# A switching LSTM's loads and stores move: waits in the relational sum, logit stores inside the recurrence, zero rows after the bases

## The chip, the core and the metric

The kernel runs on one core of a Trainium2 chip. The metric is the device time of one execution in microseconds (us). The engines are PE (TensorE), DVE (VectorE), ACT (ScalarE), POOL (GpSimd) and SP (SyncE). ACT, SP and POOL each have a queue on which they issue transfers (DMAs); an engine works through its instructions in the order in which they stand on it.

## The reference

A graph of 625 nodes with 512 features each and 20,000 edges goes through four pairs of layers. Each layer's result is added to x after a layer norm of its input. Cut to the layers in which the change lies:

```python
# layer 2, graph part: relational convolution, 32 relations out of 8 bases
weight = jnp.einsum('rb,bio->rio', w_comp, bases)
h_rel = jnp.einsum('ni,rio->rno', x, weight)
msg = h_rel[etype, src] * norm
out = jax.ops.segment_sum(msg, dst, num_segments=n_nodes) + h_bias

# layer 2, second part: a switching LSTM over the nodes, one step per node
def step(carry, x_t):
    h, c = carry
    logits = jnp.concatenate([h, c, x_t], axis=-1) @ W_sel.T + b_sel
    onehot = jax.nn.one_hot(jnp.argmax(logits, axis=-1), 4)
    ...      # the step's gates use W_ih, W_hh and the biases of the chosen one of 4 sets
    h, c = _lstm_activate(gates, c)
    return (h, c), h
```

Which of the four weight sets a step uses is known only once the step before it is done. The other layers are a Chebyshev convolution with 16 top-1 experts (layer 0), a graph convolution with a top-k expert choice (layer 1), and two attention layers with a routed attention (layer 3).

## The kernel before

The nodes lie in 5 tiles of 125 (P = 125, NT = 5), the features in 4 blocks of 128 (DC = 4), the edges in 160 chunks of 125 (EC = 160). The stages run one after the other: `setup` with `graph`, then l0_gnn, l0_ffn, l1_gnn, l1_ffn, l2_gnn, l2_ffn, l3_gnn, l3_ffn. The code is written against a framework that turns the traced instructions into one queue for each engine, gives every tile its place in its pool and adds the semaphores that data dependencies need. The order on an engine need not be the order in the code: an instruction whose inputs and tile are ready can be placed ahead of others. A `tile_critical` section is one unit to it: inside, the kernel sets its own semaphores and order. An engine takes part in a section when the section has instructions for it.

**Start.** `setup` loads x (SP, L72), makes constants on POOL, opens a DRAM tile `gxp` of 625 x 4 x 3 x 2074 bf16, and calls `graph`, which loads the edge lists and counts edges in a section of DVE, ACT and PE. Then fifteen stores on POOL (L92) write zeros into the last 26 columns of three of the four blocks of gxp, for 125 rows each.

**l1_ffn.** `self.bases`, 8 MB for l2_gnn, is loaded by eight DMAs on ACT (L471) at the stage's head; the gate weight `gw` (L477) and the experts on SP.

**l2_gnn, the relational sum.** PE makes h_rel for every node and relation; SP stores it into a DRAM table (L643, L647). Then the pool `whh` is opened (32 KB of each partition for each of the 4 weight sets), bias and row numbers are made, x gets its bias (L668), and the sum runs in a section (L684): for each chunk POOL gathers 125 rows of the table into one of 6 slots of `msg` (L688), DVE makes the one-hot matrix `dst_w` (L692), PE adds the product to the accumulators of the nodes' tiles (`chunks`, L216). `s_out` counts PE's finished passes: a chunk's gather waits until the chunk 6 places before it is through. In this section are POOL, DVE and PE.

**l2_ffn, ahead of the recurrence.** x times W_ih for all four sets is made tile by tile: `load` brings W_ih in parts of 1 MB on ACT (L750) into the place of the last weight set; `load_set` brings W_hh on SP (L707), the last set on POOL. Each result, cut into three bf16 summands, is stored to gxp (`gxo`, SP, L860). The part of the choice that depends on x alone is made into `xl3` and stored by five DMAs on ACT (L878) into the last 26 columns of block 0. `wl` (pool `cell_wl`) holds the weights of the choice and stays through the recurrence; the pools of `gin` are given back before it.

**The recurrence.** DVE sets its tiles up (L924 to L941). Then one section runs 625 steps: SP loads the step's row of gxp into `gs` (L1092) when `s_free` says that gs is free; PE adds gs into three gate banks (`inputs`, L955), multiplies the weights of the chosen set with h (`state`, L964) and sums the logits (L1024); DVE and ACT make the new c and h and the index of the largest logit; PE branches on it. POOL has no part in it.

Of the kernel before, what the change touches and what calls it, by code (L numbers as in the profile page):

```python
# [8 lines left out]
F32 = mybir.dt.float32  # L9
F16 = mybir.dt.float16  # L10
BF16 = mybir.dt.bfloat16
# [9 lines left out]
D = 512  # L21
E = 20000
P = 125
NT = N // P
DC = D // 128
# [4 lines left out]
class _Kernel:  # L30
# [36 lines left out]
    def setup(self, ctx):  # L67
        tc, nc, a = self.tc, self.nc, self.a
        const = self.const = ctx.enter_context(tc.tile_pool(name="const", bufs=1))
        self.dram = ctx.enter_context(tc.tile_pool(name="dram", bufs=1, space=DRAM))  # L70
        self.x = const.tile([P, NT, D], F32, name="x")
        nc.sync.dma_start(self.x, a["x"].rearrange("(t p) c -> p t c", p=P))  # L72
        self.ident = const.tile([128, 128], F32, name="ident")
        make_identity(nc, self.ident)
        self.eps = const.tile([P, 1], F32, name="eps")
        nc.vector.memset(self.eps, 1e-5)
        self.ones = const.tile([128, 128], F32, name="ones")
        nc.vector.memset(self.ones, 1.0)

        self.iota = const.tile([P, N], F16, name="iota")  # L80
        nc.gpsimd.iota(self.iota, pattern=[[1, N]], base=0, channel_multiplier=0,
                       allow_small_or_imprecise_dtypes=True)
        self.node = const.tile([P, NT], F32, name="node")
        nc.gpsimd.iota(self.node, pattern=[[P, NT]], base=0, channel_multiplier=1,
                       allow_small_or_imprecise_dtypes=True)
        self.gxp = self.dram.tile([N, DC, 3, 2074], BF16, name="gxp")
        zero = const.tile([P, DC - 1, 3, 26], BF16, name="zero")
        nc.gpsimd.memset(zero, 0.0)
        self.graph()
        for t in range(NT):  # L90
            for j in range(1, DC):
                nc.gpsimd.dma_start(self.gxp[t * P : (t + 1) * P, j, :, 2048:], zero[:, j - 1])  # L92

    def graph(self):

# [366 lines left out]
    def l1_ffn(self):  # L462
        tc, nc, a, x = self.tc, self.nc, self.a, self.x
# [5 lines left out]
        self.bases = bpool.tile([128, 8, DC, D], F32, name="bases")  # L469
        for b in range(8):  # L470
            nc.scalar.dma_start(self.bases[:, b], a["L2_gnn_bases"][b].rearrange("(c p) o -> p c o", p=128))  # L471
        with ExitStack() as ctx:
            pool = ctx.enter_context(tc.tile_pool(name="ec", bufs=1))
            p2 = ctx.enter_context(tc.tile_pool(name="ec2", bufs=2))
# [29 lines left out]
            g = pool.tile([P, NT, NE], F32, name="gates")  # L504
# [26 lines left out]
            for e in range(NE):  # L531
                pr = psum.tile([P, 1024], F32, name="row_ps", bufs=1)
                for t in range(NT):
                    o = t * P if t < 4 else 512
# [16 lines left out]
            free = pool.tile([P, NT, NE], F32, name="free")  # L551
# [11 lines left out]
            held = [(e, t) for e in range(EARLY) for t in range(NT)]  # L563
            for e, t, ps in products(range(EARLY, NE)):
                add(e, t, ps)
                for _ in range(2):
                    if held:
                        e, t = held.pop(0)
# [3 lines left out]
    def l2_gnn(self):  # L572


        tc, nc, a, x = self.tc, self.nc, self.a, self.x
        R, NB = 32, 8
        table = self.dram.tile([N * R, D], F32, name="rel_table")
        with self.rel as ctx:
            bases = self.bases
            pool = ctx.enter_context(tc.tile_pool(name="rg", bufs=1))  # L580
# [12 lines left out]
            with tc.tile_pool(name="rg_ln", bufs=1) as lp, tc.tile_pool(  # L593
                name="rg_tr", bufs=2, space=PSUM
            ) as psum:
                self.transpose_nodes(self.layer_norm(lp), xT, psum)
            with tc.tile_pool(name="rg_psb", bufs=2, space=PSUM) as psb, tc.tile_pool(
                name="rg_psc", bufs=3, space=PSUM
# [62 lines left out]
        with tc.tile_pool(name="rs", bufs=1) as pool:  # L661
            bias = self.bias_row(pool, "L2_gnn_h_bias")
            row = pool.tile([P, EC], F32, name="row_f")
            idx = pool.tile([P, EC], I32, name="row_i")
            nc.vector.scalar_tensor_tensor(row, self.src, float(R), self.type, op0=ALU.mult, op1=ALU.add)
            nc.vector.tensor_copy(idx, row)
            for t in range(NT):
                nc.vector.tensor_add(x[:, t, :], x[:, t, :], bias)  # L668
            with tc.tile_pool(name="rel_in", bufs=1) as sp, tc.tile_pool(
                name="rel_ps", bufs=1, space=PSUM  # L670
            ) as psum:
                NS = 6
                acc = [psum.tile([P, D], F32, name=f"acc{t}") for t in range(NT)]
                for ps in acc:
                    nc.vector.memset(ps, 0.0)
                msg = sp.tile([P, NS, D], F32, name="msg")
                d1 = sp.tile([P, NS, N], F32, name="dst_w")
                s_dve, s_out = (tc.alloc_semaphore("rel_" + n) for n in ("dve", "out"))
                s_msg = [tc.alloc_semaphore(f"rel_msg{i}") for i in range(NS)]

                def passes(slot, t):
                    yield d1[:, slot, t * P : (t + 1) * P], msg[:, slot, :], acc[t]

                with tc.tile_critical():  # L684
                    self.chunks(NS, [(lambda s: s_dve, 1, False), (lambda s: s_msg[s], 16, True)], passes, s_out)
                    for c in range(EC):
                        i = c % NS
                        get = nc.gpsimd.indirect_dma_start(  # L688
                            out=msg[:, i, :], out_offset=None, in_=table,
                            in_offset=bass.IndirectOffsetOnAxis(ap=idx[:, c : c + 1], axis=0),  # L690
                        )
                        hot = nc.vector.tensor_scalar(d1[:, i, :], self.iota, self.dst[:, c : c + 1],  # L692
                                                      self.ew1[:, c : c + 1], op0=ALU.is_equal, op1=ALU.mult)
                        if c >= NS:
                            get.wait_op(s_out, c - NS + 1, "sem-ge")
                            hot.wait_op(s_out, c - NS + 1, "sem-ge")
                        get.then_inc(s_msg[i], 16)
                        hot.then_inc(s_dve)
                for t in range(NT):
                    nc.vector.tensor_add(x[:, t, :], acc[t], x[:, t, :])  # L700
# [11 lines left out]
    def l2_ffn(self):  # L712
        tc, nc, a, x = self.tc, self.nc, self.a, self.x
        S, ROW, LG = 4, 2074, 5
        with self.cell as ctx:
# [3 lines left out]
            gxp = self.gxp  # L719
            bias3 = self.dram.tile([3, 4 * S * D], BF16, name="bias3")  # L720

            wl = ctx.enter_context(tc.tile_pool(name="cell_wl", bufs=1)).tile([128, 2, DC, S], F32, name="wl")
            wt = a["L2_ffn_W_sel"]
            for v in range(2):
                for j in range(DC):
# [5 lines left out]
            with ExitStack() as gin:  # L731
                pool = gin.enter_context(tc.tile_pool(name="gin", bufs=1))
                p2 = gin.enter_context(tc.tile_pool(name="gin2", bufs=2))

                def summands(out, value, rest):

                    nc.scalar.copy(out(0), value)
                    nc.vector.tensor_sub(rest, value, out(0))
                    nc.scalar.copy(out(1), rest)
                    nc.vector.tensor_sub(out(2), rest, out(1))  # L740
# [37 lines left out]
                with tc.tile_pool(name="gin_ln", bufs=1) as lp, tc.tile_pool(  # L778
                    name="gin_tr", bufs=2, space=PSUM
# [91 lines left out]
                    xls[:, :, 1:, :S], nxt_ps, bsel[:, None, None, :].to_broadcast([P, NT, S, S])  # L871
                )
                less = pool.tile([P, NT, 1 + S, LG], F32, name="less")
                xl3 = pool.tile([P, 3, NT, ROW - 4 * D], BF16, name="xl3")
                nc.vector.memset(xl3, 0.0)
                summands(lambda q: xl3[:, q, :, : (1 + S) * LG], xls.rearrange("p t s k -> p t (s k)"), less.rearrange("p t s k -> p t (s k)"))
                for t in range(NT):
                    nc.scalar.dma_start(gxp[t * P : (t + 1) * P, 0, :, 4 * D :], xl3[:, :, t])  # L878
            hist = self.recurrence(ctx, wl, gxp)
            psum = ctx.enter_context(tc.tile_pool(name="hb_ps", bufs=2, space=PSUM))  # L880
            for t in range(NT):
                ps = psum.tile([P, DC, 128], F32, name="h_ps")
# [5 lines left out]
                    x[:, t, :].rearrange("p (j b n) -> p b j n", j=DC, b=DC),  # L888
                )

    def recurrence(self, ctx, wl, gxp):

# [3 lines left out]
        tc, nc = self.tc, self.nc  # L898
        S, ROW, LG = 4, 2074, 5
        PE, DVE, ACT, SP = nc.tensor, nc.vector, nc.scalar, nc.sync  # L900
# [5 lines left out]
        so, tcn, h, pa = f("so", DC), f("tcn", DC), f("h", DC), f("pa", LG)  # L906
        tif, tg, to = f("tif", 256), f("tg", 128), f("to", 128)
        lm = f("lm", S, 2, DC)
        hist = f("hist", N, DC)
        mx = st.tile([2, 8], F32, name="mx")  # L910
        ix = st.tile([2, 8], U32, name="ix")
# [9 lines left out]
        lg = psum.tile([2, D], F32, name="logits")  # L921
# [17 lines left out]
        for z in (sd, gc, cc):  # L939
            nc.vector.memset(z, 0.0)  # L940
        nc.vector.memset(lg[:, :8], -3.0e38)  # L941
        c = cc[:, :, 1]
        sem = lambda n: tc.alloc_semaphore("cell_" + n)
        s_gx, s_free, s_if, s_g, s_o, s_lg, s_act, s_v, s_c, s_h, s_m, s_pa, s_ix = (
            sem(n) for n in "gx free if g o lg act v c h m pa ix".split()
        )
        banks = ((IF, 0, 256, s_if), (G, 384, D, s_g), (O, 256, 384, s_o))

        def after(ins, s, value):
            return ins.wait_op(s, value, "sem-ge")  # L950
# [27 lines left out]
        with tc.tile_critical():  # L978
# [87 lines left out]
            for t in range(N):  # L1066
# [20 lines left out]
                if t < N - 1:  # L1087
                    after(DVE.max(mx, lg[:, :8]), s_lg, t + 1).then_inc(s_ix)  # L1088
                    after(DVE.max_index(ix, mx, lg[:, :8]), s_ix, 2 * t + 1).then_inc(s_ix)

            for t in range(N):
                d = SP.dma_start(gs[: 3 * DC, :], gxp[t].rearrange("j q g -> (j q) g"))  # L1092
                if t:
                    after(d, s_free, t)
                d.then_inc(s_gx, 16)
# [324 lines left out]
```

## Time and profile before

| | |
|---|---|
| median of 4 runs | 5777.38 us (5775.17 to 5778.71) |
| profiled execution | 5783.66 us, span 5781.5 us |
| mean granted TensorE clock | 0.941 |
| busy: PE, PEld, DVE, ACT, POOL | 88%, 53%, 44%, 16%, 7% of the span |
| recurrence | about 1968 to 5104 us |
| relational sum, first to last gather | 1303.87 to 1557.6 us |

The profile shows one execution. PE is TensorE's matmuls, PEld its weight loads; a q behind an engine's name is its sequencer, which issues DMAs. "out<-in" names the tiles, L12 is line 12 of the kernel. Idle time in brackets is the time just before an instruction, with the one whose end released it.

### The profile page before, as it was taken

The numbers are of one execution on the slowest core, as the hardware profiler recorded it, in microseconds if no ns is written. First come the engines' busy times: TensorE is split into PE (matmuls) and PEld (weight loads), VectorE is DVE, ScalarE is ACT, GpSimd is POOL, SyncE is SP. The second block draws the span as 40 slices with busy tenths as digits, with TensorE's granted clock in tenths as the row PEclk, the third lists the DMA queues.
The fourth block names the chain that finished last, engine by engine and source line by source line (L and its number), as shares of the span: only waits on it lengthen the run. The fifth ranks groups of instructions, "written<-read, shape, count | busy, mean of one in ns | idle before, by whom it ended". The sixth has DMA issues, their size and how long they took to land.

```text
span 5781.5 us, 172968 instructions
## 1 busy us (share of the span) xinstructions
PE 5100.2 (88%) x74237; PEld 3074.4 (53%) x74238; DVE 2532.6 (44%) x10372; ACT 950.6 (16%) x3292; POOL 422.7 (7%) x361
## 2 busy tenths in 40 slices
PE   6898879866799699898999999999998998978898
PEld 2444764321344366565666666666665665645544
DVE  6312346324433344444454445445554443474322
ACT  1000001120033211111111111111111111133221
POOL 1000750007600000000000000000000000000000
PEclk8798999989899899999999999999999999989876
DMA  1100121496654300000000000000000000010000
GB/s 14 46 29 14 43 91 44 127 272 161 152 148 152 81 10 11 10 11 10 10 11 10 10 11 11 11 10 11 11 11 10 11 10 9 11 63 15 31 0 9
DMA packets 153757, 247.90 MB, mean 43 GB/s; under 512 B 58876, under 2 KB 61573, under 8 KB 151463
## 3 DMA queue, kind: packets, MB, share of 16 engines
q1 hardware_dynamic: 83850, 163.27, 9.6%
q0 software_dynamic: 50288, 56.13, 3.9%
q10 hardware_dynamic: 19372, 25.52, 1.5%
q8 instruction: 117, 1.92, 0.2%
q14 instruction: 130, 1.06, 0.1%
HBM read 160.50 MB, written 73.72 MB: 41 GB/s over the span
## 4 chain that ended last, share of the span: by engine, by line
PE 51%; DVE 6%; issue 3%; DMA 3%; PEld 1%; ACT 1%; PEldq 0%; SPq 0%; DVEq 0%; ACTq 0%
PE gate_if L964 20%; PE gate_o L964 9%; PE gate_g L964 8%; DMA gs<-gxp 3%; DVE to L1076 3%; PE gate_if L955 3%; PE o_ps L1203 2%; PE o_ps L1137 2%; PE idle L972 2%; PE big_ps L1339 1%; PE big_ps L1353 1%; PE blk_ps L1254 1%; PEld gate_if L964 1%; PE big_ps L1323 1%; PE fc_ps L1243 1%
## 5 line engine op out<-in xcount | busy, mean ns | idle before, releaser
L964 PE MATMUL gate_if<-whh,h 128*32 128x256 f32 x21664 | 1349.8, 387 | 2.1 <-issue 2.0
L964 PEld LDWEIGHTS gate_if<-whh,h 128*32 128x32 f32 x21664 | 599.9, 109 | 369.2 <-DVE h L1080 129.2
L964 PE MATMUL gate_g<-whh,h 128*32 128x128 f32 x19968 | 672.9, 275 | 0.0
L964 PE MATMUL gate_o<-whh,h 128*32 128x128 f32 x19968 | 660.4, 273 | 0.0
L1067 DVE STREAM_TRANSPOSE tif<-gate_if 128x256 f32<-128x256 f32 x625 | 281.3, 450 | 842.4 <-PE gate_g L964 838.7
L964 PEld LDWEIGHTS gate_g<-whh,h 128*32 128x32 f32 x19968 | 521.5, 110 | 172.8 <-issue 163.9
L964 PEld LDWEIGHTS gate_o<-whh,h 128*32 128x32 f32 x19968 | 558.6, 110 | 0.0
L1059 ACT ACTIVATE sd<-tif 128x8 f32<-128x8 f32 x625 | 135.0, 216 | 2125.3 <-DVE tif L1067 2125.3
L955 PE MATMUL gate_if<-gs,pick 128*128 128x256 bf16 x678 | 192.5, 284 | 128.6 <-DVE to L1076 30.9
L847 PE MATMUL gx_ps<-whh,xT 128*125 128x512 f32 x640 | 299.8, 612 | 0.3 <-DVE xls L787 0.3
L216 PE MATMUL acc<-msg,dst_w 125*125 125x512 f32 x352 | 187.5, 636 | 106.7 <-DMA msg<-rel_table,row_i 96.8
L1068 DVE STREAM_TRANSPOSE tg<-gate_g 128x128 f32<-128x128 f32 x625 | 197.9, 317 | 160.4 <-PE gate_g L964 160.4
L258 PE MATMUL acc<-msg,dst_w 125*125 125x128 f32 x1600 | 209.5, 281 | 45.3 <-DMA msg<-conv_table,src_i 41.5
L250 POOL DMA_INDIRECT msg<-conv_table,src_i x160 | 196.2, 1227 | 610.5 <-issue 607.4
L688 POOL DMA_INDIRECT msg<-rel_table,row_i x160 | 195.9, 1224 | 532.9 <-issue 519.3
L1076 DVE STREAM_TRANSPOSE to<-gate_o 128x128 f32<-128x128 f32 x625 | 198.2, 317 | 67.2
L1024 PE MATMUL logits<-gs,three 128*2 128x5 bf16 x624 | 103.5, 166 | 139.0 <-DMA gs<-gxp 55.5
L258 PEld LDWEIGHTS acc<-msg,dst_w 125*125 125x125 f32 x1600 | 188.0, 190 | 66.8 <-issue 54.7
L1088 DVE MAX8 mx<-logits 2x8 f32<-2x8 f32 x624 | 101.8, 163 | 246.3 <-PE logits L1036 246.3
L1024 PEld LDWEIGHTS logits<-gs,three 128*2 128x2 bf16 x624 | 49.4, 79 | 299.8 <-DMA gs<-gxp 239.7
L972 PE MATMUL idle<-hot 128*128 128x384 bf16 x624 | 204.5, 328 | 0.0
L847 PEld LDWEIGHTS gx_ps<-whh,xT 128*125 128x125 f32 x640 | 115.5, 191 | 128.0 <-issue 127.7
(350 smaller groups left out, 6238.6 us busy)
## 6 DMA issues: line engine op xcount, KB each, us to landing
rel_table<-h_rel SPq DMA_DIRECT2D x39, 1024.0 KB
gs<-gxp SPq DMA_DIRECT2D x625, 48.6 KB
gxp<-gxo SPq DMA_DIRECT2D x40, 750.0 KB
whh<-in_L_ffn_W_ih ACTq DMA_DIRECT2D x16, 1024.0 KB
whh<-in_L_ffn_W_hh SPq DMA_DIRECT2D x12, 1024.0 KB
node_basis<-by_basis SPq DMA_DIRECT2D x39, 256.0 KB
ch_wk<-in_L_gnn_weight SPq DMA_DIRECT2D x8, 1024.0 KB
expert<-in_L_ffn_experts SPq DMA_DIRECT2D x8, 1024.0 KB
```

The source lines that it names most:

```text
L216: m = PE.matmul(out, lhs, rhs, start=False, stop=False, skip_group_check=True)
L250: nc.gpsimd.indirect_dma_start(out=m, out_offset=None, in_=table, in_offset=bass.IndirectOffsetOnAxis(ap=index[:, c : c + 1], axis=0),)
L258: nc.tensor.matmul(acc[t][:, :width], w1[:, t * P : (t + 1) * P], m, start=c == 0, stop=c == EC - 1)
L688: get = nc.gpsimd.indirect_dma_start(out=msg[:, i, :], out_offset=None, in_=table, in_offset=bass.IndirectOffsetOnAxis(ap=idx[:, c : c + 1 ...
L847: nc.tensor.matmul(ps[:, q], xT[:, k, t * P : (t + 1) * P], w[:, q, k, :], start=k == 0, stop=False)
L955: m = PE.matmul(out[:, : hi - lo], pick, gs[:, s * D + lo : s * D + hi], start=True, stop=last, skip_group_check=True)
L964: yield PE.matmul(out[32 * j : 32 * j + 32, : hi - lo], h[:, b : b + 1].to_broadcast([128, 32]), self.whh[s][:, b, j, lo:hi], start=False, ...
L972: PE.matmul(idle[:, :cols], hot[:, :128], hot[:, :cols], start=True, stop=True)
L1024: after(PE.matmul(lg[:, :LG], three[:, 0], gs[:, S * D : S * D + LG], start=True, stop=False), s_gx, rows)
L1067: after(DVE.transpose(tif, IF[:, :256]), s_if, t + 1).then_inc(s_v)
L1068: after(DVE.transpose(tg, G[:, :128]), s_g, t + 1).then_inc(s_v)
L1076: after(DVE.transpose(to, O[:, :128]), s_o, t + 1).then_inc(s_v)
```

## The change

Three edits. (1) In the section of the relational sum ACT and SP get one instruction each: a wait until `s_out` is 8. (2) xl3 is made in the pool `cell_wl`, which stays open through the recurrence, and its five stores go from ACT, ahead of the recurrence, to POOL, inside the section; each waits for the store before it, and SP waits at steps 0, 125, 250, 375 and 500 for the store that covers the next 125 rows. (3) The fifteen zero stores are written behind the loads of the bases in l1_ffn. Nothing else differs.

```diff
--- before.py
+++ after.py
@@ -84,12 +84,9 @@
         nc.gpsimd.iota(self.node, pattern=[[P, NT]], base=0, channel_multiplier=1,
                        allow_small_or_imprecise_dtypes=True)
         self.gxp = self.dram.tile([N, DC, 3, 2074], BF16, name="gxp")
-        zero = const.tile([P, DC - 1, 3, 26], BF16, name="zero")
-        nc.gpsimd.memset(zero, 0.0)
+        self.zero = const.tile([P, DC - 1, 3, 26], BF16, name="zero")
+        nc.gpsimd.memset(self.zero, 0.0)
         self.graph()
-        for t in range(NT):
-            for j in range(1, DC):
-                nc.gpsimd.dma_start(self.gxp[t * P : (t + 1) * P, j, :, 2048:], zero[:, j - 1])
 
     def graph(self):
 
@@ -469,6 +466,9 @@
         self.bases = bpool.tile([128, 8, DC, D], F32, name="bases")
         for b in range(8):
             nc.scalar.dma_start(self.bases[:, b], a["L2_gnn_bases"][b].rearrange("(c p) o -> p c o", p=128))
+        for t in range(NT):
+            for j in range(1, DC):
+                nc.gpsimd.dma_start(self.gxp[t * P : (t + 1) * P, j, :, 2048:], self.zero[:, j - 1])
         with ExitStack() as ctx:
             pool = ctx.enter_context(tc.tile_pool(name="ec", bufs=1))
             p2 = ctx.enter_context(tc.tile_pool(name="ec2", bufs=2))
@@ -683,6 +683,9 @@
 
                 with tc.tile_critical():
                     self.chunks(NS, [(lambda s: s_dve, 1, False), (lambda s: s_msg[s], 16, True)], passes, s_out)
+
+                    nc.scalar.wait_ge(s_out, 8)
+                    nc.sync.wait_ge(s_out, 8)
                     for c in range(EC):
                         i = c % NS
                         get = nc.gpsimd.indirect_dma_start(
@@ -719,7 +722,9 @@
             gxp = self.gxp
             bias3 = self.dram.tile([3, 4 * S * D], BF16, name="bias3")
 
-            wl = ctx.enter_context(tc.tile_pool(name="cell_wl", bufs=1)).tile([128, 2, DC, S], F32, name="wl")
+            held = ctx.enter_context(tc.tile_pool(name="cell_wl", bufs=1))
+            wl = held.tile([128, 2, DC, S], F32, name="wl")
+            xl3 = held.tile([P, 3, NT, ROW - 4 * D], BF16, name="xl3")
             wt = a["L2_ffn_W_sel"]
             for v in range(2):
                 for j in range(DC):
@@ -871,12 +876,9 @@
                     xls[:, :, 1:, :S], nxt_ps, bsel[:, None, None, :].to_broadcast([P, NT, S, S])
                 )
                 less = pool.tile([P, NT, 1 + S, LG], F32, name="less")
-                xl3 = pool.tile([P, 3, NT, ROW - 4 * D], BF16, name="xl3")
                 nc.vector.memset(xl3, 0.0)
                 summands(lambda q: xl3[:, q, :, : (1 + S) * LG], xls.rearrange("p t s k -> p t (s k)"), less.rearrange("p t s k -> p t (s k)"))
-                for t in range(NT):
-                    nc.scalar.dma_start(gxp[t * P : (t + 1) * P, 0, :, 4 * D :], xl3[:, :, t])
-            hist = self.recurrence(ctx, wl, gxp)
+            hist = self.recurrence(ctx, wl, gxp, xl3)
             psum = ctx.enter_context(tc.tile_pool(name="hb_ps", bufs=2, space=PSUM))
             for t in range(NT):
                 ps = psum.tile([P, DC, 128], F32, name="h_ps")
@@ -888,7 +890,7 @@
                     x[:, t, :].rearrange("p (j b n) -> p b j n", j=DC, b=DC),
                 )
 
-    def recurrence(self, ctx, wl, gxp):
+    def recurrence(self, ctx, wl, gxp, xl3):
 
 
 
@@ -941,8 +943,8 @@
         nc.vector.memset(lg[:, :8], -3.0e38)
         c = cc[:, :, 1]
         sem = lambda n: tc.alloc_semaphore("cell_" + n)
-        s_gx, s_free, s_if, s_g, s_o, s_lg, s_act, s_v, s_c, s_h, s_m, s_pa, s_ix = (
-            sem(n) for n in "gx free if g o lg act v c h m pa ix".split()
+        s_gx, s_free, s_if, s_g, s_o, s_lg, s_act, s_v, s_c, s_h, s_m, s_pa, s_ix, s_xl = (
+            sem(n) for n in "gx free if g o lg act v c h m pa ix xl".split()
         )
         banks = ((IF, 0, 256, s_if), (G, 384, D, s_g), (O, 256, 384, s_o))
 
@@ -1088,7 +1090,14 @@
                     after(DVE.max(mx, lg[:, :8]), s_lg, t + 1).then_inc(s_ix)
                     after(DVE.max_index(ix, mx, lg[:, :8]), s_ix, 2 * t + 1).then_inc(s_ix)
 
+            for t in range(NT):
+                d = nc.gpsimd.dma_start(gxp[t * P : (t + 1) * P, 0, :, 4 * D :], xl3[:, :, t])
+                if t:
+                    after(d, s_xl, 16 * t)
+                d.then_inc(s_xl, 16)
             for t in range(N):
+                if t % P == 0:
+                    SP.wait_ge(s_xl, 16 * (t // P + 1))
                 d = SP.dma_start(gs[: 3 * DC, :], gxp[t].rearrange("j q g -> (j q) g"))
                 if t:
                     after(d, s_free, t)
```

## The prediction

> **What bounds the kernel now.** I read the cores view first (one core, span 5781.5 us, mean granted clock 0.941), then the chain that ended last, then the timeline, the windows and the sources around the three places that the diff touches: the start, the l2_gnn stage near 1270 us, and the hand-over to the recurrence near 1945 us. The second line is the chain by engine, the third by line.
>
> ```profile
> span 5781.5 us, 172968 instructions
> PE 51%; DVE 6%; issue 3%; DMA 3%; PEld 1%; ACT 1%; PEldq 0%; SPq 0%; DVEq 0%; ACTq 0%
> PE gate_if L964 20%; PE gate_o L964 9%; PE gate_g L964 8%; DMA gs<-gxp 3%; DVE to L1076 3%; PE gate_if L955 3%; PE o_ps L1203 2%; PE o_ps L1137 2%; PE idle L972 2%; PE big_ps L1339 1%; PE big_ps L1353 1%; PE blk_ps L1254 1%; PEld gate_if L964 1%; PE big_ps L1323 1%; PE fc_ps L1243 1%
> ```
>
> More than a third of the chain is the gate products of the 625 recurrent steps (1968 to 5104 us, 5.0 us a step). The diff removes no arithmetic from them. What it can win lies in three stalls outside; what it can lose lies in the gs loads, which are on the chain at 3%.
>
> **Part A: ACT and SP wait inside the relational sum.** In the timeline each line has start, duration, engine, line, operation, and in brackets the idle time before it and what ended it.
>
> ```profile
> 1269.64 10.15 ACTq L750 DMA_DIRECT2D whh<-in_L_ffn_W_ih  x4
> 1270.58 1.03 SPq L265 DMA_DIRECT2D bias<-in_L_gnn_h_bias  x1
> 1271.79 16.40 SPq L707 DMA_DIRECT2D whh<-in_L_ffn_W_hh  x2
> 1285.88 3.10 DVE L668 TENSOR_TENSOR x<-x,bias 125x512 f32<-125x512 f32 x5 [12.75 <-DMA bias<-in_L_gnn_h_bias]
> 1303.19 3.52 DVE L692 TENSOR_SCALAR dst_w<-iota,dst,ew 125x625 f32<-125x625 f16 x6 [14.22 <-DMA whh<-in_L_ffn_W_ih]
> 1303.87 1.51 POOL L688 DMA_INDIRECT msg<-rel_table,row_i  x1 [475.05 <-issue]
> ...
> 1309.99 4.74 PE L216 MATMUL acc<-msg,dst_w 125*125 125x512 f32 x6 [41.01 <-DMA msg<-rel_table,row_i]
> ```
>
> Six weight loads, 1 MB each, written behind the sum, are issued ahead of it. The small bias load queues beside them and lands at 1285.88; DVE waits 12.75 us for it; then the section waits another 14.22 us for the last W_ih load, though it reads none of these weights. PE stands 41.01 us for the first message.
>
> If the loads go behind the new waits, this is the sum. The last table store is issued at 1270.13 and queue traffic shows the table written by about 1273. The bias row, issued at 1270.58 on the same queue, then lands at about 1275 to 1277 instead of 1285.88: 9 to 11 us earlier. The five adds take 3.10 us and end at 1278 to 1280; entering the section cost 1.4 us between the last landing (1302.49 by its semaphore) and the first gather. So the first gather starts near 1281 instead of 1303.87: −23, of which 14.2 is the least, since that wait names the load itself. POOL, at about 1.5 us a gather, sets the pace from there to 1557.6, so an earlier start is an earlier end.
>
> Against it stand the loads, now beside the gathers. Each window line has its length, five engines' busy time, the granted clock, the DMA share and GB/s.
>
> ```profile
> 845.00:860.00 15.00, 4.65 (x22) 4.30 (x22) 5.09 (x10) 0.30 (x1) 0.00 (x0) 0.50 1.03 379
> ...
> 1340.00:1400.00 60.00, 43.33 (x81) 11.71 (x80) 27.32 (x40) 0.00 (x0) 47.78 (x41) 1.00 0.64 170
> ```
>
> Gathers alone take 0.64 of the transfer engines. Some 4.2 MB at the 379 GB/s of the fullest window are 11 us of transfer: the bound if gathers stand still meanwhile. The spare 0.36 of 379 is 137 GB/s, so the loads need some 31 us beside the gathers, and six message slots cover a longer landing (5.2/5.7/6.8 us in the rows); then the cost is 0. I take 4, nearer to nothing, because POOL's issue is the pace. Two more engines have to enter the section; I allow 1. Net A: −23 + 4 + 1 = **−18**, between −14.2 + 11 = −3 and −23. Queued behind the waits on ACT are the four W_ih loads and later stage work that began at 1570.51; on SP the W_hh loads, bb and wsel at 1564. The first user of W_ih is a matmul after 1585, 290 us later: that cover makes their lateness free; without it four loads cost the 11 us again.
>
> **Part B: the five logit stores go from ACT, ahead of the recurrence, to POOL inside it, each step block waiting for its own.**
>
> ```profile
> 1943.82 0.25 SPq L860 DMA_DIRECT2D gxp<-gxo  x1
> 1945.29 16.07 ACTq L878 DMA_DIRECT2D gxp<-xl  x5
> 1964.95 0.17 DVE L924 TENSOR_REDUCE quarter<-ident 128x4 f32<-128x12 f32 x1 [19.70 <-DMA gxp<-xl]
> 1968.39 3.01 SPq L1092 DMA_DIRECT2D gs<-gxp  x2
> 1970.42 0.40 PE L955 MATMUL gate_if<-gs,pick 128*128 128x256 bf16 x1 [27.17 <-DMA gs<-gxp]
> ```
>
> Removed: five ACT issues (16.07 us) and DVE's 19.70 us wait, after which its set-up runs 1964.95 to 1967.2. What is late next: the last gxo store, issued 1943.82, lands only at 1960.79 by its semaphore, behind the POOL weight loads. The set-up moves to 1945 to 1948, hidden in that wait. Added: POOL must enter the section (about 1 us, as at the gathers, so its first store is at 1962.7), store, and release SP. The nearest row is the zero stores: POOL stores into the same tensor, same row shape, 1.29 us an issue:
>
> ```profile
> L92 POOL DMA_DIRECT2D gxp<-zero x15: 1292/1292/1464, 2.5 to 20.8; - x15
> DMA to landing us min/median/max: 4.3/6.8/8.3
> ```
>
> The fifteen queue on each other; one alone is nearest to their minimum, 4.3. The first gs load is then at about 1967.1 instead of 1968.39: **−1.3**; at 8.3 it is 1971, +2.6. The other four stores, chained, need 4 × 4.3 to 4 × 8.3 us, done before step 8 of 125; SP's later four waits are met, nothing each. Queued behind SP's first wait is every gs load, for which PE waits.
>
> The Trainium skill, "DMA: Bandwidth & Descriptors", section "SWDGE vs HWDGE vs iDMA", speaks against this part: it puts plain transfers on SP or ACT, whose set-up is faster, and keeps GpSimd for irregular ones. By the same page's "Anatomy of one DMA — SWDGE (gpsimd) path", an estimate for 19 KB is 2.0 us fixed and 0.04 for the bytes; B would be −3.5 by it. The row of 4.3 to 8.3 decides here.
>
> **Part C: fifteen zero stores are written after the loads of the bases instead of after graph().** They are issued now at the start, though written behind the graph section:
>
> ```profile
> 2.54 19.55 POOL L92 DMA_DIRECT2D gxp<-zero  x15 [0.31 <-POOL zero L88]
> 508.48 0.37 SPq L477 DMA_DIRECT2D gw<-in_L_ffn_gate_weight  x1
> ```
>
> POOL has nothing else then, and the second line shows a load of l1_ffn issued two stages early: program order does not hold an idle queue back. I take **0**. Were they moved, the start would gain up to 7 (DVE waited 7.0 us for src_raw, the largest single wait there), and the bases stage, already at share 1.03, would lose up to the 15 × 19 KB stores' own some 9 us of transfer time: −7 to +9.
>
> **The sum.** −18 − 1.3 + 0 = −19.3 on the profiled execution: 5783.66 to 5764.4 (2.16 of it outside the span). The profiled execution is 6.28 above the median of the runs, 5777.38, so that becomes 5758. Its own range, from −23 − 3 to −3 + 2.6, is 5751 to 5777 (−3 for B if the store lands about as fast as the gs loads, near 2 us). A measurement of this kernel can tell about 0.2% (11.6 us) from no change.
>
> **The rivals.**
> *The loads overtake the waits.* For: the six loads were already issued before a section written ahead of them, as were the zero rows and gw; the order in a queue follows readiness, and ACT is free at 1269.64 while the table is still being stored. Against: in each of these the queue had no part in the section overtaken (ACT and SP in the relational sum, POOL in graph()); on engines that do take part (POOL's wl loads, issued 1564.48, SP's loads after the recurrence) nothing written behind a section stands ahead of it. Then A is 0, or −4 if only the second W_hh load, issued at 1287.86, falls behind; with B the time is 5772 to 5780, most likely 5776. Chance 0.28.
> *The zero rows move after all.* Without the hold, B with −7 to +9 gives 5769 to 5785, all within 0.2%. Chance 0.05.
> *Slower: the gs load of each step takes longer.* xl3 now stays allocated through the recurrence, so every cell tile, gs among them, lies elsewhere, and SP's stream has waits among its loads. Each step exposes that load's latency:
>
> ```profile
> PEld logits L1024 <- DMA gs<-gxp: 239.7, 563, 2.3
> ```
>
> (sum, times, longest). 625 steps turn 18.5 ns a load, 1% of a landing near 2 us, into 11.6 us: from there it decides against the no-hold case, from 50 ns against the hold. At 70 ns it is +44 − 19 = +25, 5802. Against it: the same bytes from the same rows by the same queue, and nothing in the trace ties a landing to a tile's place. Chance 0.19.
>
> **How the numbers follow.** The hold works: 0.48, the likeliest, of it 0.44 faster by more than 0.2% and 0.04 within (its weak end). Overtaken: 0.28, and zero rows: 0.05, all within. Slower rival: 0.19, of it 0.18 beyond. Together 0.44 faster, 0.38 within, 0.18 slower. The range 5751 to 5795 leaves out the stronger part of the slower rival, from some 60 ns with the hold (0.13), and the tail below (0.05).
>
> **What would show it.** Right: W_ih issued after the first matmul of the sum, first gather near 1281, the bias wait below 3 us, the last gather near 1536; zero stores still at 2.5 us; first gs load near 1949; 5.0 us a step. Wrong: W_ih on ACT ahead of the first gather and its wait of 14 us kept (the first rival), or an unchanged start of the sum with another sum of the waits on gs (the last).

## The result and the profile after

The changed kernel takes 5783.4 us (median of 32 runs) against 5778.9 us of the kernel before (52 runs): ratio 1.0009, 95% interval 1.0004 to 1.0014, that is 2 to 8 us slower. The forecast was 5758 us and faster. The profiled execution after took 5790.05 us (span 5788.2, clock 0.939), 6.4 above the one before.

The page after, span and chain by engine; this chain was followed back through the stages ahead of the recurrence as well, so its shares add up to more than those before, but the gate products at L966 have 20, 9 and 9% (20, 9 and 8% before):

```profile
span 5788.2 us, 173011 instructions
PE 71%; DVE 8%; issue 7%; DMA 7%; POOL 3%; ACT 1%; PEld 1%; PEldq 0%; ACTq 0%; SPq 0%; POOLq 0%; DVEq 0%
```

The timeline after, around the relational sum, at the place of the lines shown of before:

```profile
1269.57 6.88 ACTq L755 DMA_DIRECT2D whh<-in_L_ffn_W_ih  x4
1270.50 1.05 SPq L262 DMA_DIRECT2D bias<-in_L_gnn_h_bias  x1
1271.73 50.92 SPq L710 DMA_DIRECT2D whh<-in_L_ffn_W_hh  x3
1285.04 3.10 DVE L668 TENSOR_TENSOR x<-x,bias 125x512 f32<-125x512 f32 x5 [11.99 <-DMA bias<-in_L_gnn_h_bias]
1303.28 3.52 DVE L695 TENSOR_SCALAR dst_w<-iota,dst,ew 125x625 f32<-125x625 f16 x6 [15.14 <-DMA whh<-in_L_ffn_W_ih]
1303.95 1.51 POOL L691 DMA_INDIRECT msg<-rel_table,row_i  x1 [474.39 <-issue]
```

The W_ih loads are where they were, on ACT, ahead of ACT's own part in the section; so are two W_hh loads, and both waits of the section's entry stand (11.99 and 15.14 us). What moved is one load: the group of W_hh now has three in it, and ends 50.92 us after its start, at 1322.65. Before, it had two by then and the third came at 1563.7, as this line of before, over a longer stretch, shows:

```profile
1271.79 292.23 SPq L707 DMA_DIRECT2D whh<-in_L_ffn_W_hh  x3
```

SP's wait for pass 8 releases that third load into the sum. The gathers after:

```profile
1329.02 1.22 POOL L691 DMA_INDIRECT msg<-rel_table,row_i  x1 [0.31 <-issue]
...
1335.28 7.24 PE L213 MATMUL acc<-msg,dst_w 125*125 125x512 f32 x12 [6.75 <-DMA msg<-rel_table,row_i]
...
1337.61 1.40 POOL L691 DMA_INDIRECT msg<-rel_table,row_i  x1 [7.37 <-PE acc L213]
```

and their source's times from issue to landing:

```profile
DMA to landing us min/median/max: 5.2/5.7/14.1
```

POOL, which issues a gather every 1.5 us, stands 7.37 us for a free slot: a gather took up to 14.1 us to land (6.8 before), PE waited 6.75 us for one, and a slot is free only when PE is through with it. In windows of before and after, in this order, with busy times, clock, DMA share and GB/s:

```profile
1320.00:1330.00 10.00, 6.96 (x13) 1.76 (x12) 4.46 (x7) 0.00 (x0) 8.16 (x7) 1.00 0.63 165
1330.00:1340.00 10.00, 7.29 (x14) 2.05 (x14) 4.07 (x7) 0.00 (x0) 7.86 (x8) 1.00 0.65 174
```

```profile
1320.00:1330.00 10.00, 5.09 (x10) 1.17 (x8) 3.49 (x5) 0.00 (x0) 8.17 (x7) 0.94 0.85 179
1330.00:1340.00 10.00, 4.72 (x7) 2.16 (x8) 1.23 (x3) 0.00 (x0) 2.33 (x3) 0.55 0.85 148
```

The share rises to 0.85, but the bytes don't: 179 and 148 GB/s against 165 and 174, with 1 MB more to move. The last gather starts at 1566.42 instead of 1556.45.

At the hand-over to the recurrence:

```profile
1971.74 1.34 POOL L1094 DMA_DIRECT2D gxp<-xl  x1 [21.05 <-issue]
1975.66 2.96 SPq L1101 DMA_DIRECT2D gs<-gxp  x2
1977.64 0.39 PE L957 MATMUL gate_if<-gs,pick 128*128 128x256 bf16 x1 [24.37 <-DMA gs<-gxp]
```

The five stores' source:

```profile
DMA to landing us min/median/max: 3.7/3.8/4.0
```

From the last gxo store's issue (1954.08; 1943.82 before) to the first gs load are 21.6 us, 24.6 before: the stores inside the recurrence gain 3.0. The zero stores have a new line and the old place (timeline), and the wait for gs in the steps is what it was (waits: sum, times, longest):

```profile
2.54 19.51 POOL L471 DMA_DIRECT2D gxp<-zero  x15 [0.31 <-POOL zero L88]
```

```profile
PEld logits L1026 <- DMA gs<-gxp: 238.6, 564, 2.4
```

### The profile page after: what moved, and what is told of

Read it like the earlier page. It is cut to its first block, busy times and chain, and to the rows that moved or that the text cites. A ratio compares the mean times of both kernels' runs of the same rounds, so it can differ in the third digit from the quotient of the medians.

```text
span 5788.2 us, 173011 instructions
## 1 busy us (share of the span) xinstructions
PE 5105.3 (88%) x74237; PEld 3078.7 (53%) x74238; DVE 2529.9 (44%) x10372; ACT 950.5 (16%) x3292; POOL 429.9 (7%) x366
## 3 DMA queue, kind: packets, MB, share of 16 engines
q10 hardware_dynamic: 17472, 25.42, 1.5%
## 4 chain that ended last, share of the span: by engine, by line
PE 71%; DVE 8%; issue 7%; DMA 7%; POOL 3%; ACT 1%; PEld 1%; PEldq 0%; ACTq 0%; SPq 0%; POOLq 0%; DVEq 0%
PE gate_if L966 20%; PE gate_o L966 9%; PE gate_g L966 9%; PE gx_ps L852 4%; DVE to L1078 3%; PE gate_if L957 3%; PE ch_b L339 3%; DMA gs<-gxp 3%; PE ch_b L330 2%; PE y_ps L608 2%; POOL msg L691 2%; PE cnt L213 2%; PE idle L974 2%; PE o_ps L1212 2%; PE o_ps L1146 2%
## 5 line engine op out<-in xcount | busy, mean ns | idle before, releaser
L966 PE MATMUL gate_if<-whh,h 128*32 128x256 f32 x21664 | 1351.6, 388 | 1.8 <-issue 1.7
L966 PEld LDWEIGHTS gate_if<-whh,h 128*32 128x32 f32 x21664 | 600.3, 109 | 369.7 <-DVE h L1082 129.2
L966 PE MATMUL gate_g<-whh,h 128*32 128x128 f32 x19968 | 674.2, 276 | 0.0
L966 PE MATMUL gate_o<-whh,h 128*32 128x128 f32 x19968 | 659.4, 273 | 0.0
L966 PEld LDWEIGHTS gate_g<-whh,h 128*32 128x32 f32 x19968 | 522.9, 110 | 171.4 <-issue 162.5
L966 PEld LDWEIGHTS gate_o<-whh,h 128*32 128x32 f32 x19968 | 557.6, 110 | 0.0
L255 PEld LDWEIGHTS acc<-msg,dst_w 125*125 125x125 f32 x1600 | 187.2, 188 | 67.5 <-issue 58.4
L1026 PEld LDWEIGHTS logits<-gs,three 128*2 128x2 bf16 x624 | 49.3, 79 | 299.3 <-DMA gs<-gxp 238.6
L213 PEld LDWEIGHTS acc<-msg,dst_w 125*125 125x125 f32 x352 | 60.6, 201 | 244.3 <-issue 189.4
```

The lines of the kernel that those rows point to most:

```text
L213: m = PE.matmul(out, lhs, rhs, start=False, stop=False, skip_group_check=True)
L255: nc.tensor.matmul(acc[t][:, :width], w1[:, t * P : (t + 1) * P], m, start=c == 0, stop=c == EC - 1)
L966: yield PE.matmul(out[32 * j : 32 * j + 32, : hi - lo], h[:, b : b + 1].to_broadcast([128, 32]), self.whh[s][:, b, j, lo:hi], start=False, ...
```

## The experiments

The theory ("L" below): the load that SP's wait lets into the sum costs it 10 us, the logit stores give 3 back, the zero rows nothing. Each profiled execution is cut at the same instructions: entry, from the last table store (L647) to the first gather; sum, from first to last gather; to gx, from there to the first matmul of x with W_ih; gx, from that to the last; hand-over, from there to the first gs load.

| kernel | entry | sum | to gx | gx | hand-over | ratio to before (95%) |
|---|---|---|---|---|---|---|
| before | 33.7 | 252.6 | 29.1 | 351.9 | 30.9 | |
| after | 33.9 | 262.5 | 28.9 | 352.3 | 28.0 | 1.0009 (1.0004 to 1.0014) |
| e1_no_waits | 33.8 | 253.2 | 28.8 | 352.2 | 27.9 | 0.9995 (0.9986 to 1.0004) |
| e3_late_wait | 33.9 | 252.6 | 30.3 | 352.1 | 28.2 | 0.9999 (0.9990 to 1.0007) |
| e5_sp_only | 34.1 | 259.9 | 28.9 | 352.1 | 27.9 | 1.0012 (1.0004 to 1.0021) |
| e6_act_only | 34.3 | 255.3 | 29.5 | 352.1 | 27.9 | 1.0000 (0.9991 to 1.0009) |
| d1_tall | 33.6 | 262.6 | 26.8 | 352.5 | 27.8 | one run |
| d2_wide | 34.7 | 258.7 | 28.9 | 352.3 | 27.9 | one run |
| e7_zero_late | 35.5 | 252.5 | 29.0 | 353.4 | 28.3 | 1.0011 (1.0003 to 1.0020) |
| e4_held | 9.2 | 253.2 | 29.4 | 361.7 | 27.8 | 0.9973 (0.9962 to 0.9983) |
| v1_held_pool | 8.6 | 253.5 | 32.3 | 354.3 | 28.4 | 0.9967 (0.9955 to 0.9980) |
| v2_held_bases | 8.2 | 253.6 | 32.3 | 370.2 | 28.2 | 0.9969 (0.9957 to 0.9981) |
| v3_held_both | 8.4 | 253.8 | 32.1 | 354.3 | 28.2 | 0.9945 (0.9931 to 0.9958) |

Stage times are of one execution each. The recurrence (first to last gs load) takes 3125 to 3134 us and what follows 677 to 685 in these kernels, in no order that follows the edits; a few us of a single span are that.

The sum can be read more finely. Counted from the first gather, the 25th starts 8.2 us later than in before in the changed kernel, 6.1 in e5, 8.2 in d1 and 4.6 in d2, the four with a load among the gathers, and within 0.5 us of before in all the others. So the load itself cost the changed kernel 8.2 of its 9.9 us. The rest came 140 us after the load: 2.0 us at the 108th gather, in a pause that every kernel has (4.2 to 4.6 us from start to start in the others, 6.3 in this one), and no run shows why.

**Without the waits.**

```diff
-                    nc.scalar.wait_ge(s_out, 8)
-                    nc.sync.wait_ge(s_out, 8)
```

> The changed kernel without the two waits in the relational sum; the logit stores on POOL stay. Theory L (the SP wait lets one W_hh load run inside the sum, and that load costs the sum 10 us, while the logit stores gain 3 us): the third W_hh load is issued near 1564 us again, behind the sum; first to last gather take 252 to 253 us as before the change (262.5 in the changed kernel); first gs load about 3 us earlier than before against the same stage's start; time about 3 us under before (ratio 0.9995). Rival S (the stores inside the recurrence are what costs, by later gs loads): the time stays about 5 us above before, the sum being 10 us shorter and the rest 10 us longer.

The SP timeline of this kernel has the third W_hh load behind the sum again (the group's end is 1561.84):

```profile
1269.24 292.60 SPq L710 DMA_DIRECT2D whh<-in_L_ffn_W_hh  x3
```

The sum is back at 253.2 with the stores still inside the recurrence and their 3 us kept: rival S falls. The median, 5773.1 against 5777.5, agrees with the 3 us, but the interval includes no change.

**The same waits, for pass 158.** `s_out, 8` becomes `s_out, 158`, in both.

> The changed kernel with both waits at 158 of the 160 passes instead of 8; the order of the instructions on each engine is the changed kernel's. Theory L: the third W_hh load is issued near 1557 us, behind the last gathers, and the sum takes 252 to 254 us; time 2 to 4 us under before. Rival W (the two engines' part in the section, their entry or their place in the code, slows the sum, not the load): the sum still takes about 262 us and the time stays about 5 us above before.

The third W_hh load of this kernel:

```profile
1566.10 0.31 SPq L710 DMA_DIRECT2D whh<-in_L_ffn_W_hh  x1
```

It is issued at 1566.1, after the last gather (1561.49), and the sum takes 252.6. Both engines have their part in the section and the order is the changed kernel's, so rival W falls: neither the entry nor the code costs, only what the wait lets go.

**One wait at a time.**

```diff
-                    nc.scalar.wait_ge(s_out, 8)
```

is taken out in e5_sp_only,

```diff
-                    nc.sync.wait_ge(s_out, 8)
```

in e6_act_only.

> The changed kernel with SP's wait alone; ACT's is taken out. Theory L: it is SP's part in the section that puts the third W_hh load directly behind its own wait, so the load is issued near 1322 us, and first to last gather take 262 us as in the changed kernel; time 4 to 7 us above before. Rival: both waits are needed, or ACT's is the one that counts; then the sum takes 253 us.

> The changed kernel with ACT's wait alone; SP's is taken out. Theory L: the third W_hh load is behind the sum again (near 1562 us), the four W_ih loads are still issued near 1270 us ahead of the section, first to last gather take 252 to 254 us, time about 3 us under before. Rival W (an engine's part in the section costs by itself): some 5 us of the 10 stay.

The W_hh group of e5_sp_only:

```profile
1272.29 50.93 SPq L710 DMA_DIRECT2D whh<-in_L_ffn_W_hh  x3
```

With SP's wait alone the third load goes at 1322.9 and the sum takes 259.9; with ACT's alone it goes at 1567.9 and the sum takes 255.3. So it is SP. In e6 the W_ih loads are at 1270.2 as always: a wait in the section doesn't hold a load written behind it, on an engine that takes part either. Of its 2 to 3 us over the others, 2 are one pause behind the 130th gather (5.6 us, 3.3 to 3.8 in the others), which no expectation covers; at the 25th gather this kernel isn't late at all.

**One more load in the sum, from another queue, in two shapes.** Based on e6_act_only, ACT behind its wait issues an extra load of 1 MB into the place of the third set (d1: `W_hh[2, 0]`, d2: a part of `W_ih`) and waits for it:

```diff
                     nc.scalar.wait_ge(s_out, 8)
+                    s_ld = tc.alloc_semaphore("rel_ld")
+                    nc.scalar.dma_start(place, source).then_inc(s_ld, 16)
+                    nc.scalar.wait_ge(s_ld, 16)
```

> e6_act_only with one more load inside the sum, on ACT behind its wait: 1 MB of W_hh in the shape of the weight loads (32 partitions, 8 KB pieces), into the place of the third set, which is loaded again later. Theory L (such a load beside the gathers costs the sum 10 us, whoever issues it): gathers 15 to 20 stall, first to last gather 261 to 264 us. Rival Q (it is SP's queue or the load's place in it that hurts): 253 to 255 us. By bytes alone (1.05 MB at the 379 GB/s of the fullest window) it would be at most 2.8 us, 256 us.

> As d1_tall, but the extra 1 MB is of W_ih in its shape (128 partitions, 2 KB pieces). If the pieces of 8 KB into 32 partitions are what holds the gathers up: the sum takes 253 to 257 us, the bytes' 2.8 us at most. If any 1 MB beside the gathers costs as much: 261 to 264 us.

The longest pause in POOL's timeline, of d1 and then of d2:

```profile
1340.98 1.42 POOL L694 DMA_INDIRECT msg<-rel_table,row_i  x1 [4.72 <-PE acc L213]
```

```profile
1343.78 1.42 POOL L694 DMA_INDIRECT msg<-rel_table,row_i  x1 [3.43 <-PE acc L213]
```

A weight load of W_hh's shape costs the sum about as much from ACT's queue as from SP's (262.6 us, 8.2 us late by the 25th gather; 6.1 and 8.2 from SP's): rival Q falls. The same megabyte in W_ih's shape makes the 25th gather 4.6 us late: less, but above the 2.8 of its bytes, and the sum of 258.7 is in neither of the two expected ranges. The longest time from a gather's issue to its landing is 14.1 us in the changed kernel, 13.0 in e5, 14.3 in d1, 10.9 in d2, and at most 7.3 in the kernels without such a load. While the tall load ran, the trace's packets, in steps of 2 us, show gathers and load together at 144 to 196 GB/s; beside the wide one, 238 to 288 at its height. Both are single runs, and the two kernels with the same load on SP differ by 2 us among themselves, so that the shape matters is likely, not shown.

The Trainium skill, "DMA: Bandwidth & Descriptors", section "Back-pressure in remote DMA", says that stalled writes hold up the other queues of the same transfer engine when a destination is saturated. That would fit 8 KB pieces into 32 partitions holding up the gathers; it is told there of transfers between cores, and no run here shows it or separates pieces from partitions.

**The hold, done so that it holds.** The pool of the weight sets is opened behind the sum; no waits.

```diff
-        self.cell = ExitStack()
-        wpool = self.cell.enter_context(tc.tile_pool(name="whh", bufs=1))
-        self.whh = {s: wpool.tile([128, DC, DC, D], F32, name=f"whh{s}") for s in range(4)}
         with tc.tile_pool(name="rs", bufs=1) as pool:
...
                     nc.vector.tensor_add(x[:, t, :], acc[t], x[:, t, :])
+        self.cell = ExitStack()
+        wpool = self.cell.enter_context(tc.tile_pool(name="whh", bufs=1))
+        self.whh = {s: wpool.tile([128, DC, DC, D], F32, name=f"whh{s}") for s in range(4)}
```

> No waits; the pool of the four weight sets is opened behind the sum instead of ahead of it, so that no W_ih or W_hh load can be issued before the sum ends; the logit stores on POOL stay. By the prediction's term for a hold: bias row lands by about 1277 us, first gather near 1281 us instead of 1304, sum of 252 us, last gather near 1533 us; W_ih is issued near 1540 us and lands by about 1560, before its first matmul would run (22 us after the sum's end in before), so the gain of 23 us stays: time 20 to 26 us under before with the stores' 3. Rival G (the loads only move their cost): the first product of x and W_ih waits for the loads, and 10 us or more of the 23 come back in that stage: time 5 to 15 us under before.

Timeline of e4_held:

```profile
1278.87 3.53 DVE L692 TENSOR_SCALAR dst_w<-iota,dst,ew 125x625 f32<-125x625 f16 x6 [5.71 <-DMA bias<-in_L_gnn_h_bias]
1279.59 1.47 POOL L688 DMA_INDIRECT msg<-rel_table,row_i  x1 [449.58 <-issue]
```

The entry falls from 33.7 to 9.2 us, 24.5; the time by 0.27%, about 16 us (median 5758.7 against 5777.5), between the two expected ranges. Not all of the 24.5 is the loads' going: the five adds of the bias, 3.1 us, stood ahead of the sum and now run behind it (in v1 to v3 too), and the first weight loads are issued at 1543.47, as these adds end:

```profile
1540.37 3.08 DVE L665 TENSOR_TENSOR x<-x,bias 125x512 f32<-125x512 f32 x5
```

The first product does not wait (29.4 us after the last gather), but the products' stage takes 361.7 instead of 352: rival G was right that some comes back, 10 us, though not where it said.

**Zero rows really late.** The zero tile goes into the pool of the bases, based on e1_no_waits:

```diff
-        self.zero = const.tile([P, DC - 1, 3, 26], BF16, name="zero")
+        self.zero = bpool.tile([P, DC - 1, 3, 26], BF16, name="zero")
```

> As e1_no_waits, and the tile of zeros lies in the pool of the bases, which opens in l1_ffn, so that the fifteen zero stores are really issued there (near 840 us) and not at 2.5 us. By the prediction's term: the start gains up to 7 us (src_raw's wait) and the bases' stage loses up to 9: time within -7 and +9 us of e1_no_waits. Theory that the start's loads are held up by the zero stores: the edge loads land earlier and the graph section begins at about 24 us instead of 30.5. Rival: the start is unchanged, since the loads' own latency sets it, and the difference to e1_no_waits is 0 to +9.

The graph section's first one-hot starts at 24.7 us instead of 31.0 in e1: the start gains 6.3, and there the first theory was right. At l1_gnn's last gather 2.1 of them are left (824.1, 826.2). Then ACT's timeline:

```profile
837.95 25.42 ACTq L468 DMA_DIRECT2D bases<-in_L_gnn_bases  x8
863.42 0.30 ACT L48 ACTIVATE ln_rs<-ln_mv,eps 125x5 f32<-125x5 f32 x1 [27.01 <-DMA bases<-in_L_gnn_bases]
```

Beside the zero stores ACT needs 25.42 us to issue the bases (13.40 in the kernel before), and the layer norm's `ln_rs` behind it starts 39.3 us after l1_gnn's last gather instead of 26.1 in e1. From that gather to the last table store it takes 454.1 instead of 441.4: 12.7 lost, and the later `ln_rs` accounts for all of it (13.2). The median is 8.8 above before and 13 above e1, beyond the +9 allowed.

**Giving back what the hold lost.** `load_set(s)` becomes `load_set(s, queue=nc.gpsimd)` for the twelve W_hh loads (v1); the bases' `nc.scalar.dma_start` becomes `nc.gpsimd.dma_start` (v2); both (v3); all on e4_held.

> e4_held with the twelve W_hh loads on POOL's queue instead of SP's. In e4_held the products of x and W_ih took 362 us from first to last instead of 352, with the W_hh loads standing among the gxo stores on SP. If SP's order is the cause, that stage goes back to 352 us and the time falls 8 to 10 us below e4_held's 5759. Rival: the twelve loads, now issued together behind the sum, crowd out the W_ih loads, the first products wait, and 0 to 20 us are lost against e4_held.

> e4_held with the eight loads of the bases on POOL's queue instead of ACT's. In the kernel before, ACT issues them for 13.4 us and the layer norm's ln_rs behind them waits 15.1 us; e7_zero_late made that 25 us and cost 12. If ACT's queue is what holds the stage, ln_rs runs at about 842 us instead of 853 and the time falls 8 to 12 us below e4_held's 5759. Rival: the experts' loads wait for the same transfer engines and the stage's end moves by less than 3 us.

> v1_held_pool and v2_held_bases together: pool of the weight sets behind the sum, W_hh and the bases on POOL's queue, logit stores on POOL. In v2_held_bases the table was stored 9 to 12 us earlier but the products of x and W_ih took 370 us, in v1_held_pool they took 354 us. If W_hh among the gxo stores on SP was what took v2's gain back, the last table store is near 1259 us, the products take 352 to 356 us, and the time is some 8 us below v1_held_pool, 28 us below before. Rival: the products stage lengthens whenever it starts earlier; then they take 360 us or more and the time stays near v1's.

v1: the products' stage goes back to 354.3, and 2.9 are lost ahead of it: both halves of the expectation came true in part, 4.5 us in the stages, and the intervals of e4 and v1 don't separate (medians 5758.7 and 5761.1). v2: `ln_rs` runs when its input is there (in before ACT's issuing held it for 15.12 us),

```profile
843.29 0.30 ACT L48 ACTIVATE ln_rs<-ln_mv,eps 125x5 f32<-125x5 f32 x1 [4.00 <-DVE ln_mv L47]
```

and the last table store comes 11.7 us earlier than in e4 (1258.7, 1270.4), but the products then take 370.2, the recurrence begins when e4's does and the time stays at e4's (median 5760.0). v3 tells these apart: with the W_hh loads off SP's queue the earlier start is kept (products 354.3) and the time is 5746.8 us, ratio 0.9945, about 32 us under before. So it was the W_hh loads among the gxo stores on SP that took v2's gain back, not the earlier start.

## Why the prediction was wrong

**The hold (the likeliest case, 0.48): its step failed, its price was nearly right.** The step was that on an engine which takes part in a section nothing written behind it would be issued ahead of it, read from POOL's wl loads and SP's loads after the recurrence. The trace of before could not show that: those loads also lie in pools that open behind their sections. ACT took part and still issued W_ih at 1269.57. So the forecast's largest term, −23, stayed away: the first gather came at 1303.95 instead of near 1281. e4_held, where the hold holds, has the first gather at 1279.59, the entry 24.5 us shorter (23 predicted; some 3 of the 24.5 are the five adds, which the prediction left ahead of the sum) and a median of 5758.7. That the last equals the forecast is part chance: 10 us went to the products' stage, which the prediction had at nothing ("that cover makes their lateness free"), and the 4 for loads beside the gathers weren't paid.

**The loads overtake (0.28): the right case, with the wrong load.** Entry and W_ih are as this rival says, at 0 for A. What it missed is that a wait not only holds loads back but also lets one go. The third W_hh load had stood on SP behind the whole section. The prediction names W_hh behind SP's wait where the hold works, but this rival, with A at 0 or −4, has no price for a load let into the sum. It runs there; the sum is 9.9 us longer, 8.2 of them by the 25th gather.

**The price of a load beside the gathers.** Taken as 4 for 4.2 MB, by a spare share of 0.36 and six slots; at most 11. (4.2 MB are the four W_ih loads; the W_hh loads, behind a wait as well by the prediction's own list, aren't in it.) One load of 1 MB cost 6 to 8 (after, e5, d1). The spare share didn't show this: the gathers landed in up to 14.1 us, more than six slots of 1.5 us cover, and POOL stood.

**Part B: right in mechanism, −3.0 instead of −1.3.** POOL's first store came 17.7 us after the last gxo store's issue (18.9 predicted) and landed in 3.8 (4.3 from the zero rows). The Trainium skill ("DMA: Bandwidth & Descriptors", section "SWDGE vs HWDGE vs iDMA") puts plain transfers on SP or ACT. Here they went from ACT to POOL and the hand-over still got shorter: only the first store is waited for there, and the waits for gs in the steps didn't grow (238.6 us against 239.7). The estimate of 2.0 us for a landing, from the same page's "Anatomy of one DMA — SWDGE (gpsimd) path", was too low by 1.8; that its sum, −3.5, was nearer than the row's is luck, since the store also went out 1.2 us sooner than predicted.

**Part C: 0, as predicted,** and its two terms, when really moved, were +12.7 and −6.3 (up to 9 and 7 predicted). The first reached the stage through ACT, held 12 us longer by its issuing, which the prediction did not name; it took the stores' own transfer time.

**The slower rival (gs loads): not seen.** Waits for gs are 238.6 us against 239.7. The kernel is slower by another way. That 5783.4 lies inside 5751 to 5795 is luck: the room at the top was left for this rival. The hold and the overtaking reach only to 5780, and the zero rows, which reach 5785, didn't move.

## What to carry to other kernels

A wait put on an engine moves whatever stands next on its queue: ask which instruction that is in the order of the queue, not in the code, and at what moment it is let go. To hold a load back, take away its place rather than put a wait ahead of it in the code; the later pool held here while the adds behind the sum were still to be done, and an order in the code alone held nothing. One 1 MB load beside this chain of paced small gathers cost 4.6 to 8.2 us, 1.6 to 2.9 times what its bytes take at the fullest rate (2.8); price such a load by landing times and free slots, not by the spare share.

## What was not expected of the hardware

A load of 1 MB into 32 partitions in 8 KB pieces took the gathers in the changed kernel from about 170 GB/s to as little as 22 GB/s for some 2 us, and slowed them for 10, while the sum of both stayed under 200 GB/s, about half of the 379 of the fullest window. And PE's granted clock was 0.55 in the window of that pause (1.00 before); the twelve matmuls that followed the pause took 0.77 us each on average, against 0.63 at the same place before. ACT took 25.42 us to issue eight loads beside the zero stores, and 13.40 without them.
